# Turning four token groups between the first maxima of a fused attention and expert block

## The chip, the cores and the metric

The kernel runs on one NeuronCore of a Trainium2 chip. The engines meant below are TensorE (PE, the matrix engine, with its weight loads PEld), VectorE (DVE), ScalarE (ACT), GpSimd (POOL) and SyncE (SP), which only issues transfers. The metric is the device time of one execution in microseconds (us). The time before is 1413.76 us, the median of three runs (1411.64 to 1413.96).

## The reference

All arrays are float32. The input is 4 sequences of 1024 tokens with 256 channels, so 4096 tokens.

```python
xn = layernorm(x)                         # no weights, eps 1e-5
qkv = xn @ W_qkv + b_qkv                  # 16 heads of 16
q, k = rope(q), rope(k)
attn = softmax(q @ k.T / 4) @ v
y_att = attn @ W_out + b_out
scores = sigmoid(xn @ w_gate.T)           # 16 experts in 4 groups
# the best 2 groups by the sum of their two best scores, in them the best 4 experts,
# weights = their scores divided by their sum
routed = sum over chosen e of weight_e * (silu(xn @ w1_e.T) * (xn @ w3_e.T)) @ w2_e.T
shared = (silu(xn @ w1_s.T) * (xn @ w3_s.T)) @ w2_s.T
out = x + y_att + routed + shared
```

## The kernel before

**Tiles and groups.** The 4096 tokens are 32 tiles of 128 tokens, and four tiles make a group q of 512 tokens; there are eight groups, q = 0 to 7, two for each sequence b. Three things are done to a group in class `Norm`. `scale(q)` (L452) normalises it in place on ScalarE, in four instructions of 128x256. `turn(q, pair)` (L467) transposes two of its tiles on TensorE, four transposes of 128x128 into one PSUM bank, and ScalarE copies that bank to the transposed activations (L489). `store(q)` (L463) writes the normalised group to DRAM. Transposed groups of sequences 2 and 3 (q = 4 to 7) have only a temporary place, in buffers with the tags `oc` and `acc`, one buffer each, shared by even and odd groups, and go to DRAM from there (L542). `gate(qs)` (L494) computes the router's logits for up to four transposed groups, and `logits_of` (L513) turns them back.

**Start.** Groups 0 and 1 are normalised by VectorE and turned first; the loop at L148 then projects sequence 0 tile by tile, rotates q and k, and turns them. In the same loop ScalarE takes the sums and sums of squares of later groups (`stats_later`, L377), and GpSimd computes their scale and offset after it (`power`, L408), in the order of q.

**First maxima.** The softmax subtracts a maximum for each query that is found beforehand: `max_one` (L1237) is a product of 32 rows into a PSUM bank and a VectorE maximum over it (L1255). Four of these, one for each head of a group of heads, make a `max_round`. For the first four heads the even rounds run inside the loop and the odd rounds at L172 to L173. `max_off` (L1262) joins the halves, transposes the maxima on TensorE (tile `pmt`) and subtracts them from the queries on VectorE. Only then can the first exponentials start.

**Steps.** The rest is a run of 256 steps (L267). A step has four products `ps` with their exponentials on ScalarE (`exp_one`, L1282) and four products `pm` with their maxima for the next four heads (`max_one`). They come in two halves. Between the halves stand the step's units (`between`, L1470), which `pieces` (L544) lists: in steps 0 to 6 a further `max_round` (two in step 6), in steps 0 to 5 the two turns of group q = step + 2, the gates in steps 3 and 5, and the turning back of their logits in steps 4 and 6. After the second half come the products `av` of the step before, whole or in halves, which the flag `more` of `step` (L1446, set at L290 from `norm.gates`) decides. `moves` (L531) is called ahead of each step: it emits `scale(step + 3)`, the store of group step + 2 and, for turned groups from 4 on, the transfer of the transposed group to DRAM.

**What sets the order.** `k.pe` and `k.sp` keep the instructions of TensorE and of SP's queue in the order in which the program is written. On the other engines an instruction is ordered among others only where `keep_in_program_order` is called: on ScalarE that is so for the sums, the copies of q and k of sequence 0, the scalings of groups 2 and 3, and some later instructions. All PSUM tiles come from one pool of eight banks (L83), so a product waits until an engine has read the bank that it takes over. Routing on VectorE and GpSimd starts at step 9 with a sigmoid over the logits (L608); the zero fills of the dispatch buffer start there too.

Of the kernel before, what the change touches and what calls it, by code (L numbers as in the profile page):

```python
# [20 lines left out]
NT = B * TT  # L21
# [7 lines left out]
HALF = 512  # L29
QT = 4  # L30
# [22 lines left out]
def kernel(  # L53
# [23 lines left out]
    nc = tc.nc  # L77
# [6 lines left out]
    k = Kit(tc, banks)  # L84
# [38 lines left out]
    norm = Norm(k, att, ff, keep, logits, power)  # L123
# [44 lines left out]
    with tc.issue_after(k.rotary):  # L168
        for power_of in powers:
            power_of()  # L170
    norm.scale(2)
    for qt in range(4):  # L172
        att.max_round(0, 0, 2 * qt + 1)  # L173
    att.max_off(0, 0, 0)

    def weights():
        nc.scalar.dma_start(out=k.w1s_sb, in_=w1s.rearrange("(c p) f -> p c f", p=P))
        nc.scalar.dma_start(out=k.w3s_sb, in_=w3s.rearrange("(c p) f -> p c f", p=P))
        nc.scalar.dma_start(out=k.w2s_sb, in_=w2s.rearrange("(c p) h -> p c h", p=P))
        k.sp(wout_sb, w_out.rearrange("(c p) f -> p c f", p=P))  # L180
# [83 lines left out]

    ex = ExitStack()
    now = pieces(0)
    for step in range(STEPS):  # L267
        beside.tick()
        norm.moves(step)
        if step in k.at_step:  # L270
            with tc.issue_after(k.last_exp):
                k.at_step[step]()

        bits = []
        if routing is not None and step >= ROUTE_FROM:
            bits += [advance] * (1 if step >= PUT_FROM else 2 if k.ranking else 3)
        if step >= PUT_FROM and beside.put_next < n_put:
            assert k.slots_known
            bits[:0] = [beside.put] * 2
        if step > done.get("tiles", STEPS):  # L280
            if beside.got == 0:
                ex.close()
                beside.rows = att.rows = ctx.enter_context(
                    tc.tile_pool(name="gp", bufs=4, side="right")
                )
            for _ in range(2 if step < STEPS - 2 * TT else 1):
                bits += [beside.get, beside.add]
        then = pieces(step + 1) if step + 1 < STEPS else []

        att.step(now, bool(then) and (step + 1 > 6 or step + 1 in norm.gates), bits)  # L290
        now = then
# [4 lines left out]
class Kit:  # L296


    def __init__(self, tc, banks):
        self.tc, self.nc, self.banks = tc, tc.nc, banks  # L300
        self.last_sp = self.last_exp = None
        self.ranking = self.slots_known = False
        self.summed = self.shared_rows = 0
# [26 lines left out]
class Norm:  # L330
# [3 lines left out]
    def __init__(self, k, att, ff, keep, logits, power):  # L334
        self.k, self.nc, self.att, self.ff = k, k.nc, att, ff
        self.logits, self.power = logits, power
        self.gates = {3: (2, 3, 4, 5), 5: (6, 7)}
        self.less = keep.tile([P, NT], F32, name="less")
        self.sq = keep.tile([P, NT], F32, name="sq")
        self.x4, self.xnT, self.part, self.lg = {}, {}, {}, {}  # L340
        self.mv, self.rstd, self.off, self.scaled = {}, {}, {}, None
# [28 lines left out]
    def power_of(self, q):  # L370
        nc, ff, mv = self.nc, self.ff, self.mv[q]
        rstd = self.rstd[q] = ff.tile([P, QT], F32, name=f"rstd_{q}", tag="rstd", bufs=8)
        keep = self.k.tc.keep_in_program_order
        keep(nc.gpsimd.tensor_scalar_add(mv[:, :, 1], mv[:, :, 1], 1e-5))
        keep(nc.gpsimd.tensor_tensor(rstd, mv[:, :, 1], self.power, ALU.pow))
# [76 lines left out]
    def scale(self, q):  # L452
        nc = self.nc
        for i in range(QT):
            x = self.x4[q][:, i, :]
            scale = nc.scalar.activation(
                x, x, AF.Identity,
                bias=self.off[q][:, i : i + 1], scale=self.rstd[q][:, i : i + 1],
            )
            if q < 4:  # L460
                self.k.tc.keep_in_program_order(scale)

    def store(self, q):  # L463
# [3 lines left out]
    def turn(self, q, pair):  # L467

        nc, k = self.nc, self.k
        b, hf = divmod(q, 2)  # L470
        if hf == 0 and pair == 0 and b < 2:
            self.xnT[b] = k.xnTp.tile([P, NC_, T], F32, name=f"xnT_{b}", tag="xnT")
        if pair == 0:
            if b < 2:
                self.part[q] = self.xnT[b][:, :, hf * HALF : (hf + 1) * HALF]
            else:

                self.part[q] = self.att.one.tile(
                    [P, NC_, HALF], F32, name=f"xnTq_{q}", tag=("oc", "acc")[hf]
                )  # L480
        pt = k.bank([P, NC_, 2, P], f"pt_{q}_{pair}")
        for i in range(2):
            for c in range(NC_):
                k.pe(
                    nc.tensor.transpose(  # L485
                        pt[:, c, i, :], self.x4[q][:, 2 * pair + i, c * P : (c + 1) * P], k.ident
                    )
                )
        nc.scalar.copy(  # L489
            self.part[q][:, :, pair * 2 * P : (pair + 1) * 2 * P],  # L490
            pt.rearrange("p c i n -> p c (i n)"),
        )

    def gate(self, qs):  # L494


        nc, k = self.nc, self.k
        ps = k.bank([P, HALF], f"pg_{qs[0]}")
        for c in range(NC_):
            for j in range(4):  # L500
                k.pe(
                    nc.tensor.matmul(
                        ps[32 * j : 32 * j + 32, :],
                        lhsT=self.wg2[:, c, :],
                        rhs=self.part[qs[j % len(qs)]][:, c, :],
                        start=(c == 0), stop=(c == NC_ - 1),
                    )
                )
        lg = self.ff.tile([P, R, C], F32, name=f"lg_{qs[0]}", tag="y", bufs=3)
        self.lg[qs] = lg.rearrange("p r c -> p (r c)")  # L510
        nc.scalar.copy(self.lg[qs], ps)
# [19 lines left out]
    def moves(self, step):  # L531

        k = self.k
        q = step + 3
        if q < NT // QT:
            with k.tc.issue_after(k.last_exp or k.pace):
                self.scale(q)
        if step + 2 < NT // QT:
            self.store(step + 2)
        if 4 <= step + 1 < NT // QT:  # L540
            b, hf = divmod(step + 1, 2)
            k.sp(k.xnTd[b][:, :, hf * HALF : (hf + 1) * HALF], self.part[step + 1])  # L542

    def pieces(self, step, own):  # L544
        out = []
        if step + 2 < NT // QT:
            out += [lambda: self.turn(step + 2, 0), lambda: self.turn(step + 2, 1)]
        if own:
            out.append(own.pop(0))
        if step in self.gates:  # L550
            out.append(lambda: self.gate(self.gates[step]))
        if step - 1 in self.gates:
            out.append(lambda: self.logits_of(self.gates[step - 1]))
        return out + own
# [239 lines left out]
class Beside:  # L794
# [167 lines left out]
    def expert_units(self, ex):  # L962
# [50 lines left out]
        def pair_of(i):  # L1013
            def run():
                if i == 0:
                    for n in range(FFN_AHEAD - 1):
                        load(n)
                    turn(0)
                if i:
                    outer(i - 1)  # L1020
                if i + FFN_AHEAD - 1 < PAIRS:
                    load(i + FFN_AHEAD - 1)
                if i + 1 < PAIRS:
                    turn(i + 1)
                gus[i] = self.hidden(xTs[i], gate_and_up(i), f"r{i}")
            return run
# [543 lines left out]
```

## Time and profile before

| What | us |
|---|---|
| median of three runs | 1413.76 |
| the profiled execution, its own time | 1414.77 |
| its span, first to last instruction | 1413.1 |
| TensorE busy | 1389.0 (98%) |
| VectorE busy | 931.0 (66%) |
| ScalarE busy | 783.6 (55%) |
| GpSimd busy | 424.7 (30%) |
| mean granted TensorE clock | 0.991 |

The change lies in the first 112 us of the span. A profile row of a group gives the line, the engine, the operation and the tiles, then busy time and mean duration. A row of the windows gives, for a stretch of the span, the time for which each engine was busy and the number of its instructions, then the granted TensorE clock (1.00 is full speed), the mean busy share of the transfer engines, and GB/s. A row of the chain of waits gives start, duration and the engine and line on the path that ended last. Products are pipelined and their ends are modelled, so a busy TensorE can still be short of work; the number of its instructions in a window says more.

### The profile page before, as it was taken

How to read it: one execution, taken by the hardware profiler on the slowest of the kernel's cores; microseconds unless marked ns; L12 is line 12 of the kernel's file. 1: busy time of each engine (PE TensorE's matmuls, PEld its weight loads, DVE VectorE, ACT ScalarE, POOL GpSimd, SP SyncE). 2: the span in 40 equal slices, each digit the busy share in tenths (PEclk: the TensorE clock that was granted, in tenths of full speed). 3: DMA queues.
4: the chain of work that ended last, by engine and by line, in shares of the span. 5: the costliest groups of instructions: out<-in, count | busy, mean ns of one | idle time of the engine just before them, and what ended most of it. 6: DMA issues, size and time to landing. Idle time of an engine off the chain costs nothing.

```text
span 1413.1 us, 25832 instructions
## 1 busy us (share of the span) xinstructions
PE 1389.0 (98%) x9446; PEld 653.6 (46%) x9446; DVE 931.0 (66%) x1734; ACT 783.6 (55%) x1586; POOL 424.7 (30%) x498
## 2 busy tenths in 40 slices
PE   7899999999999999999999999999999999999998
PEld 4443333343343335566566665665664333333333
DVE  6778758778777765444555555555447988998941
ACT  4564445565555555555555555555555555555575
POOL 5401603764444454220000000002225444444400
PEclk9899999999999999999999999999999999999999
DMA  5143743413332333547666666665432434433310
GB/s 187 45 150 134 283 165 104 142 68 105 120 120 104 99 135 95 172 153 230 210 203 201 202 202 213 197 200 174 150 120 75 125 107 128 127 108 105 109 38 31
DMA packets 136670, 199.10 MB, mean 141 GB/s; under 512 B 13920, under 2 KB 99040, under 8 KB 136288
## 3 DMA queue, kind: packets, MB, share of 16 engines
q1 hardware_dynamic: 103088, 137.78, 30.7%
q0 software_dynamic: 12288, 33.57, 7.7%
q10 hardware_dynamic: 21168, 26.10, 5.3%
q8 instruction: 75, 1.23, 0.4%
q14 instruction: 51, 0.42, 0.1%
HBM read 124.01 MB, written 79.69 MB: 144 GB/s over the span
## 4 chain that ended last, share of the span: by engine, by line
PE 97%; DVE 1%; DMA 1%; ACT 1%; issue 0%; POOL 0%; ACTq 0%; POOLq 0%; DVEq 0%
PE ps L1289 20%; PE pm L1247 20%; PE av L1314 18%; PE ph_r L827 9%; PE exy L994 5%; PE ph_s L859 5%; PE pqk L1161 4%; PE py L1383 2%; PE pso L899 2%; PE pv L1161 2%; PE ext L985 2%; PE ptr L1228 2%; PE pmt L1270 1%; PE po L1338 1%; DVE mx L1255 1%; PE pt L485 1%
## 5 line engine op out<-in xcount | busy, mean ns | idle before, releaser
L1298 ACT ACTIVATE es<-ps 128x512 f32<-128x512 f32 x1024 | 554.9, 596 | 460.3 <-PE ps L1289 238.4
L1255 DVE TENSOR_REDUCE mx<-pm 128x1 f32<-128x512 f32 x1024 | 661.3, 685 | 193.9 <-PE pm L1247 139.0
L1247 PE MATMUL pm<-kT,qT 32*128 32x512 f32 x1792 | 513.1, 646 | 1.4 <-ACT kT L1233 1.4
L1289 PE MATMUL ps<-q,kT 32*128 32x512 f32 x1792 | 509.3, 643 | 3.1 <-DVE mx L1255 2.2
L1314 PE MATMUL av<-es,vv 128*32 128x512 f32 (+1 forms) x2144 | 277.3, 588 | 0.0
L1289 PEld LDWEIGHTS ps<-q,kT 32*128 32x128 f32 x1792 | 142.5, 184 | 192.5 <-ACT es L1298 135.0
L1247 PEld LDWEIGHTS pm<-kT,qT 32*128 32x128 f32 x1792 | 147.5, 185 | 67.6 <-DVE mx L1255 30.0
L835 DVE SCALAR_TENSOR_TENSOR th_r<-th_r,ph_r 128x256 f32<-128x256 f32 x72 | 30.3, 421 | 199.6 <-ACT th_r L834 199.6
L950 POOL DMA_INDIRECT xs<-rows,slot_i x128 | 124.0, 969 | 114.7 <-DVE mx L1255 101.5
L1042 POOL DMA_INDIRECT yg<-ys,slot_i x128 | 121.5, 949 | 121.8 <-DVE mx L1255 115.8
L1192 POOL TENSOR_TENSOR rot<-qk,sin_sb 128x256 f32<-128x256 f32 x56 | 39.5, 728 | 348.4 <-DVE qk L1149 348.2
L827 PE MATMUL ph_r<-xT,w 128*128 128x128 f32 x1152 | 140.5, 275 | 0.5 <-ACT xT L988 0.5
L1314 PEld LDWEIGHTS av<-es,vv 128*32 128x32 f32 x2144 | 43.1, 108 | 199.9 <-issue 178.1
L827 PEld LDWEIGHTS ph_r<-xT,w 128*128 128x128 f32 x1152 | 134.4, 192 | 0.8 <-ACT xT L988 0.7
L994 PE MATMUL exy<-w,gu_r 128*128 128x256 f32 x288 | 76.6, 388 | 0.0
L834 ACT ACTIVATE th_r<-ph_r 128x256 f32<-128x256 f32 x72 | 27.7, 384 | 82.6 <-PE ph_r L827 82.6
L1289 PE MATMUL ps<-q,qkT 32*128 32x512 f32 x256 | 72.7, 640 | 0.0
L1247 PE MATMUL pm<-qkT,qkT 32*128 32x512 f32 x256 | 72.6, 640 | 0.0
L994 PEld LDWEIGHTS exy<-w,gu_r 128*128 128x128 f32 x288 | 50.6, 190 | 28.9 <-issue 21.7
L1059 DVE SCALAR_TENSOR_TENSOR sum<-yg,wk,sum 128x256 f32<-128x256 f32 x128 | 63.6, 496 | 0.4 <-DMA yg<-ys,slot_i 0.4
L1000 ACT ACTIVATE y<-exy 128x512 f32<-128x512 f32 x72 | 43.2, 600 | 35.0 <-PE exy L994 29.9
L875 POOL TENSOR_TENSOR xb<-xb,bo_sb 128x512 f32<-128x512 f32 x16 | 20.9, 1308 | 90.4 <-DMA xb<-in_x_dram 76.4
(178 smaller groups left out, 1210.3 us busy)
## 6 DMA issues: line engine op xcount, KB each, us to landing
w<-we SPq DMA_DIRECT2D x144, 384.0 KB, 3.8
xs<-zero ACTq DMA_DIRECT2D x8, 2304.0 KB, 7.9
xg<-xs SPq DMA_DIRECT2D x72, 256.0 KB, 4.8
ys<-y SPq DMA_DIRECT2D x72, 256.0 KB, 4.7
acc<-acc SPq DMA_DIRECT2D x14, 512.0 KB, 5.2
xb<-in_x_dram SPq DMA_DIRECT2D x16, 256.0 KB, 4.2
acc<-xb SPq DMA_DIRECT2D x16, 256.0 KB, 3.2
we<-in_w_dram ACTq DMA_DIRECT2D x4, 1024.0 KB, 7.3
```

Of the source, the lines that this page charges most:

```text
L827: nc.tensor.matmul(ph[:, n, at], lhsT=w[n][:, c, :], rhs=xT[:, c, at], start=(c == 0), stop=(c == NC_ - 1),)
L859: nc.tensor.matmul(ph, lhsT=w[:, i, c * P : (c + 1) * P], rhs=self.xnT[b][:, i, at : at + SL], start=(i == 0), stop=(i == NC_ - 1),)
L950: put = nc.gpsimd.indirect_dma_start(out=k.xs, out_offset=bass.IndirectOffsetOnAxis(ap=k.slot_i[:, t, kk : kk + 1], axis=0), in_=self.rows ...
L994: nc.tensor.matmul(py[:, r, :], lhsT=gus[i][:, r * P : (r + 1) * P], rhs=got[i][1][:, r, 2 * NC_ * F :], start=True, stop=True,)
L1042: get = nc.gpsimd.indirect_dma_start(out=self.yg[:, kk, :], out_offset=None, in_=k.ys, in_offset=bass.IndirectOffsetOnAxis(ap=k.slot_i[:, ...
L1059: nc.vector.scalar_tensor_tensor(sm[:, 0, :], yg[:, kk, :], k.wk[:, t, kk : kk + 1], sm[:, 0, :], ALU.mult, ALU.add)
L1161: nc.tensor.matmul(ps, lhsT=self.xnT[b][:, c, t * P : (t + 1) * P], rhs=self.wqkv_sb[:, c, at : at + w], start=(c == 0), stop=(c == NC_ - 1),)
L1247: nc.tensor.matmul(ps, lhsT=self.qT[b, g // 2][rows, g % 2, qt * P : (qt + 1) * P], rhs=self.kT[b, g // 2][rows, g % 2, hf * HALF : (hf + ...
L1255: k.pace = nc.vector.tensor_reduce(out=self.mx_of[b, g, qt // 4][hf][:, qt % 4, j, :], in_=ps, axis=AX.X, op=ALU.max,).ins
L1289: nc.tensor.matmul(ps, lhsT=self.kT[b, g // 2][rows, g % 2, kc * P : (kc + 1) * P], rhs=self.q2[b, g, qh][rows, :], start=True, stop=True,)
L1298: k.last_exp = nc.scalar.activation(e, ps, AF.Exp, scale=DH**-0.5).ins
L1314: nc.tensor.matmul(av[32 * j : 32 * j + 32, cols], lhsT=self.vv[b][:, kc, h * VS : h * VS + 32], rhs=es[j][:, cols], start=(kc == 0), stop ...
```

## The change

Groups 2 to 5 are turned between the odd maximum rounds, ahead of the first step, and no longer in steps 0 to 3. For that their scalings come there too. Groups 6 and 7, formerly turned in steps 4 and 5, are turned in steps 2 and 3, and are scaled from steps 0 and 1. The gate over groups 2 to 5 moves from step 3 to step 1 and that over 6 and 7 from step 5 to step 4; turning back the logits follows one step later each. The scalings of groups up to 5 and the copies of the turns of groups 2 to 5 are kept in written order on ScalarE. `moves` keeps its stores of groups in the same steps; the transfers of transposed groups 4 and 5 are emitted in steps 0 and 1, those of 6 and 7 in steps 3 and 4.

```diff
     norm.scale(2)
+    norm.scale(3)
+
     for qt in range(4):
         att.max_round(0, 0, 2 * qt + 1)
+        if qt == 1:
+            norm.turn(2, 0)
+            norm.scale(4)
+        if qt == 2:
+            norm.turn(2, 1)
+    for q in (3, 4):
+        for pair in range(2):
+            norm.turn(q, pair)
+    norm.scale(5)
     att.max_off(0, 0, 0)
+    for pair in range(2):
+        norm.turn(5, pair)
...
-        self.gates = {3: (2, 3, 4, 5), 5: (6, 7)}
+
+        self.turns, self.gates = {2: 6, 3: 7}, {1: (2, 3, 4, 5), 4: (6, 7)}
...
-            if q < 4:
+            if q < 6:
                 self.k.tc.keep_in_program_order(scale)
...
-        nc.scalar.copy(
+        copy = nc.scalar.copy(
             self.part[q][:, :, pair * 2 * P : (pair + 1) * 2 * P],
             pt.rearrange("p c i n -> p c (i n)"),
         )
+        if 2 <= q < 6:
+            k.tc.keep_in_program_order(copy)
...
-        q = step + 3
+        q = step + 6
         if q < NT // QT:
             with k.tc.issue_after(k.last_exp or k.pace):
                 self.scale(q)
         if step + 2 < NT // QT:
             self.store(step + 2)
-        if 4 <= step + 1 < NT // QT:
-            b, hf = divmod(step + 1, 2)
-            k.sp(k.xnTd[b][:, :, hf * HALF : (hf + 1) * HALF], self.part[step + 1])
+        q = step + 4 if step < 2 else self.turns.get(step - 1)
+        if q:
+            b, hf = divmod(q, 2)
+            k.sp(k.xnTd[b][:, :, hf * HALF : (hf + 1) * HALF], self.part[q])
...
-        if step + 2 < NT // QT:
-            out += [lambda: self.turn(step + 2, 0), lambda: self.turn(step + 2, 1)]
+        if step in self.turns:
+            out += [lambda i=i: self.turn(self.turns[step], i) for i in range(2)]
```

## The prediction

> **What bounds the kernel now.** I read the page's rows by slices first (a dip in TensorE's clock in slices 2 and 4), then the chain of waits from 46 us on, then the windows, and last the timelines of the engines up to 112 us. Rows of the chain, with start and duration:
>
> ```profile
> 49.20 9.65 DVE mx L1255 x16
> ...
> 59.12 1.13 PE pmt L1270 x4
> ...
> 60.34 0.70 DVE q L1275
> ...
> 61.08 1.22 PE ps L1289
> ...
> 63.17 1.90 PE pt L485 x8
> 65.07 2.63 PE pm L1247 x9
> ```
>
> To be seen: before the first step VectorE's sixteen odd maxima (0.604 us each) set the end for 9.65 us, and TensorE waits. From 61.08 on TensorE is the path, and the turns are pieces of it: 1.90 us in step 0, then 1.02 to 1.03 in each of steps 1 to 5 (rows at 70.77, 77.15, 83.52, 90.72 and 98.43). The change moves turns from the second stretch into the first. The windows show a second loss. I cut them at 3.41 us because the six jumps of the clock up to 180 us (53.65, 67.3, 128.8, 135.6, 176.6, 180.0) lie whole multiples of that apart.
>
> ```profile
> 46.82:50.24 3.42, 2.22 (x17) 1.01 (x18) 2.26 (x5) 3.42 (x11) 3.09 (x14) 1.00 0.00 0
> 50.24:53.65 3.41, 3.41 (x13) 1.60 (x12) 3.41 (x7) 1.94 (x4) 3.19 (x22) 1.00 0.61 207
> 53.65:57.06 3.41, 2.53 (x5) 0.72 (x4) 3.41 (x7) 0.00 (x0) 3.00 (x8) 0.51 0.62 183
> 57.06:60.48 3.42, 1.12 (x4) 0.72 (x4) 2.11 (x5) 0.00 (x0) 0.67 (x2) 0.50 0.00 0
> 60.48:63.89 3.41, 2.81 (x12) 1.30 (x13) 1.21 (x3) 0.70 (x2) 0.00 (x0) 0.50 0.00 0
> 63.89:67.30 3.41, 3.41 (x18) 2.00 (x20) 0.82 (x3) 1.54 (x3) 0.00 (x0) 0.50 0.00 0
> 67.30:70.72 3.42, 3.42 (x17) 1.20 (x9) 3.42 (x7) 2.51 (x6) 0.00 (x0) 0.99 0.29 79
> ```
>
> The first pair behind the stretch's length is TensorE, busy time and instructions; the first number after the last bracket is the granted clock. With 13 starved matmuls in a window the clock falls to half; it stays there for four windows, which hold the pmt transposes and nearly all of step 0.
>
> **Part 1, the entry.** TensorE's added work is the turns of groups 2 to 5: 32 transposes, eight in 1.02 us, 4.1 us. All but those of group 5 are hidden under the 9.65 us of maxima. Do they starve VectorE through the eight banks? The product of maximum 14 would take over the bank of turn (2,0). ScalarE copies that bank behind eight scalings of 0.515 us (timeline: eight in 4.12 us from 48.06), so it is free at 52.8. I put the product at 54.0, and its maximum is due at 57.7: no stall. If a copy were 4 us later there would be one.
>
> ScalarE now has a chain of its own: 16 scalings (8.2 us) and eight copies (0.54 to 0.59 us, 4.5 us), from 48.06 to 60.8 if nothing gaps. Placed link by link: the copies of groups 3 and 4 end about 58.2 (their turns get banks as maxima 9 to 11 end, 55.2 to 56.4), and group 5's scaling runs to 60.3. TensorE in its fixed order does pmt at 59.12, 0.6 us at full clock, then turn (5,0), waits until 60.3, does turn (5,1) and is free at 60.85. So the wait on ScalarE takes the place of the half-speed pmt (1.13 us) and the subtraction behind it (0.70): first ps at 60.9 against 61.08. Queued behind that wait are all of step 0's products, hence the exponentials and VectorE.
>
> The unknown here is where ScalarE's scaling of group 6 lands: it is not kept in order and step 0's pace is a VectorE instruction. Behind the first exponentials it costs nothing; ahead of group 5's it costs four scalings, 2.06 us (a turn can't be late by more). Its nearest row is group 3's scaling, emitted in the same way in step 0 before, but kept in order, and that ran far ahead. I take 0 and keep 2.06 for the range. Its offset is no limit: GpSimd has it at 56.2, group 4's at 52.6, and 4 is scaled at 52.8.
>
> **Part 2, step 0.** Before, the first maximum started at 63.23, 2.15 us after the first product, and the tenth ended at 71.99, with VectorE idle for 2.59 us in between. At full clock the same product-to-maximum delay was 1.20 us (75.69 to 76.89). Afterwards: 60.9 + 1.20 = 62.1, then ten maxima back to back (1.29 + 4.88 us by VectorE's rows) end at 68.25. TensorE's products for them come to about 4.6 us, so VectorE paces. Gain **3.7 us**. Of this the turn's 1.90 us is one part and the clock the rest; neither adds in full, because VectorE is next.
>
> **Part 3, steps 1 to 6.** Five turns were left there, two remain: 3 x 1.02 = **3.1 us** off TensorE's path. Gates (1.85 us each) and logits (0.59 us each) are moved only; they count the same before and after. Can VectorE follow? Between 72 and 111 us its waits on TensorE are 5.7 + 3.5 = 9.2 us, so a saving of 3.1 has room. If steps without any extra unit are held up by VectorE (eight maxima, 4.9 us) a third of it is lost, 1 us; if the better spread of gates helps, 0.5 more comes.
>
> **Part 4, what costs nothing, and its cover.** On SP's queue the transfer of transposed group 4 now waits for a copy at 58.2, and group 3's store, group 5's transfer, w_out and group 4's store queue behind it. Such a transfer lands in 3.0 to 3.9 us; w_out is first read at 120.77, and the temporary buffer of group 4, needed again by group 6 in step 2, is read out by about 62 and by the gate in step 1. Without that cover turn 6 would wait. The stores of x that free these buffers first were issued at 14.4 and 15.9. Logits done a step sooner bring nothing: the first reader is the sigmoid at 122.76. From step 7 on instructions, their order and the zero fills are placed by step number, so the rest moves as a block; the path there is TensorE nearly everywhere.
>
> **Sum.** 3.7 + 3.1 = 6.8 us off the profiled execution's own 1414.77, i.e. 1407.97. That execution was 1.0 above the median 1413.76, so the forecast for a median is 1413.76 - 6.8 = **1407.0**.
>
> **A rule against the change.** Part of the gain needs the clock to stay up while TensorE transposes. First the row: the window 63.89:67.30 restored the clock at its end, though turns fill it until 65.07, that is 35% of it. The window before it, idle until 61.08 (17%), did not, nor did 128.74:132.16, which had no full-array transposes and was filled from 129.5 on (78%). So 65% of other work restored what 78% could not: transposes must count. The Trainium skill, "TensorE: Matmul & The Clock Gate", Part 4: PE-mode transpose, says the opposite: full clock does not engage for transposes, which do not count as busy in the same way. By the rule the clock falls at about 53.65 as before, the turns take 8 us in the entry, first ps comes near 62.3, step 0 runs at half speed as before, and only its turn and the three later ones are won: 1.90 + 3.1 - 1.2 = 3.8 us, 1410.0. By the row 1407.0. I go with the row, since the filled windows 50.24 and 53.65 would get eight and sixteen transposes more; 57.06:60.48 with some eight or twelve in all stays doubtful, and a fall there would cost at most 1.7 us.
>
> **Rivals.**
>
> (B) *Smaller gain, 1410.0.* The clock falls before step 0 after all, by the rule above, or group 6's scaling comes first (6.8 - 2.1 = 4.7, so 1409.1). For it: the skill, and the unordered scaling. Against it: the windows.
>
> (C) *Slower, 1417.2.* Clock falls in steps 0 to 6. There TensorE, once ahead of VectorE, waits for banks: twelve products, 24 matmuls, in 4.9 us make about 16.7 a window. At 17 the clock stayed, at 13 it fell; the skill's page, "A second HAM failure mode: psum-queue depth-cycling", describes such oscillation. A fall lasts two windows (128.8 to 135.6) and costs half of 6.8 us, 3.4. Two falls give back the gain; from three it is slower: -6.8 + 3 x 3.4 = +3.4. Against it: gates, turns and av fill TensorE in steps 1 to 6, and in the window 104.85:108.26, paced by VectorE with 20 matmuls, the clock stayed.
>
> (D) *No change, 1413.8.* The gain is lost at a fixed transfer further on: the chain has 6.92 us from 164.83 for loading xb. If the load ended at a set time, all 6.8 us would go there. Against it: the load is issued by its step, as are the fills beside it.
>
> (E) *The turns are not out of the path*, because they starve the maxima: 4.1 us back into the entry, 1411.1. Against it: the bank count of part 1.
>
> **How the numbers follow.** Forecast 0.60, B 0.16, E 0.03, D 0.09, C 0.12. A measurement of this kernel can tell about 0.2%, 2.8 us, from no change: faster means below 1410.9, slower above 1416.6. Faster: the forecast and most of B, 0.74. Same: D, E and the rest of B, 0.14. Slower: C, 0.12. The range: the forecast's own bounds are 6.8 + 0.5, and 6.8 - 2.1 - 1.0; the clock's falls at 128.8 and 176.6 cost 3.4 and 1.7 us and may not recur, since the shift puts other work into those windows. So down to 1403.5. Up I go to 1412.0, which takes in B and E and leaves out C and D.
>
> **What would show it.** Right: maxima L1255 still unbroken for 9.65 us from about 49.2; turns L485 of groups 2 to 4 inside it; clock 1.00 from 50 to 68; first ps at 60.5 to 61.5; VectorE unbroken for its first ten maxima of the steps; step 7 about 6.8 us sooner, and the same lead at the end. Wrong: gaps in the maxima (E), half clock between 53 and 68 (B) or again up to 110 (C), first ps after 62.5 (group 6 first), a lead that vanishes between 120 and 180 (D).

## The result: slower, with the profile after

The changed kernel takes 1419.45 us (median of five runs, 1417.33 to 1422.17) against 1411.78 for the kernel before (now five runs, 1411.53 to 1413.96). The ratio is 1.0046 (1.0032 to 1.0061). The forecast was 1407.0 with a range of 1403.5 to 1412.0; the kernel got slower, not faster. Ratios are given with their 95% intervals and can differ in the last digits from the quotient of the two medians. The profiled execution took 1417.33 us; its span is 1415.6.

The place to look is the same stretch as before. First the chain of waits of the changed kernel up to the first products of the odd rounds (start, duration, engine, line):

```profile
51.36 0.97 POOL rstd L389
...
53.95 0.97 POOL rstd L433
...
55.55 1.02 POOL rstd L433
...
56.64 0.21 POOL off L435
...
56.87 1.09 ACT x L470 x2
57.96 0.52 ACT qT L1250 x2
58.49 0.55 ACT kT L1250 x2
...
60.02 0.97 ACT x L470 x2
...
61.85 3.80 PE pm L1264 x16
```

Before, this stretch of the path belonged to VectorE's maxima. Now GpSimd is on it, which the forecast had set aside ("Its offset is no limit"): it computes the scale and offset of one group after another (L389, L433, L435), and as soon as the offset of group 6 is there, ScalarE scales `x`, that is group 6, and only then copies q and k. ScalarE's timeline (start, duration, then idle time before the row and what ended it) says why:

```profile
45.24 0.51 ACT L413 ACTIVATE other<-x,less 128x256 f32<-128x256 f32 x1
45.64 0.20 ACT L413 ACTIVATION_READ_ACCUMULATOR other<-x,less 128x1 f32 x1
56.87 1.09 ACT L470 ACTIVATE x<-x,off,rstd 128x256 f32<-128x256 f32 x2 [11.03 <-POOL off L435]
57.87 0.62 ACT L1250 COPY qT<-ptr 128x256 f32<-128x256 f32 x2
58.38 0.65 ACT L1250 COPY kT<-ptr 128x256 f32<-128x256 f32 x2
...
61.93 4.07 ACT L470 ACTIVATE qkT<-qkT,off,rstd 128x256 f32<-128x256 f32 x8
```

In the kernel before, nothing stood between the squares and those copies, and the scalings of groups 2 and 3 followed them:

```profile
47.54 0.71 ACT L1233 COPY kT<-ptr 128x256 f32<-128x256 f32 x2
48.06 4.12 ACT L456 ACTIVATE qkT<-qkT,off,rstd 128x256 f32<-128x256 f32 x8
```

In the changed kernel one half of group 6's scaling stands ahead of the copies of q and k of each of the last two tiles of sequence 0. ScalarE does nothing for 11.03 us, although the transposes that those copies read were done by 47.4. The list of waits shows what hung on it (waiting engine and line, engine waited for, total, times, longest):

```profile
DVE mx L1272 <- PE pm L1264: 15.2, 1, 15.2
PEld pm L1264 <- ACT kT L1250: 14.7, 1, 14.7
PE pm L1264 <- ACT kT L1250: 14.4, 1, 14.4
ACT x L470 <- POOL off L435: 11.0, 1, 11.0
```

TensorE can't start the odd rounds without k, and VectorE can't take maxima. The sixteen maxima themselves are as unbroken as before, only later, and so is the start of the steps (VectorE's timeline):

```profile
63.96 9.66 DVE L1272 TENSOR_REDUCE mx<-pm 128x1 f32<-128x512 f32 x16 [15.16 <-PE pm L1264]
...
74.66 0.69 DVE L1292 TENSOR_TENSOR q<-qT,pmt 128x512 f32<-128x512 f32 x1 [0.82 <-PE pmt L1287]
76.86 8.46 DVE L1272 TENSOR_REDUCE mx<-pm 128x1 f32<-128x512 f32 x14 [1.51 <-PE pm L1264]
```

The odd maxima start at 63.96 and not at 49.18. After that what the forecast spoke of is there: fourteen maxima without a gap, where the kernel before had gaps of 2.59 and 0.90 us:

```profile
67.11 4.88 DVE L1255 TENSOR_REDUCE mx<-pm 128x1 f32<-128x512 f32 x8 [2.59 <-PE pm L1247]
72.89 3.68 DVE L1255 TENSOR_REDUCE mx<-pm 128x1 f32<-128x512 f32 x6 [0.90 <-PE pm L1247]
```

The subtraction of the maxima from the queries (L1292 here, L1275 before) comes 32 times in the run and serves as a time mark for comparing executions. The table has its start in each profiled execution, as a distance from the kernel before; the experiments are described below.

| subtraction | before, us | changed | keep6 | late67 | early6 | power6 | dummy | dummy2 |
|---|---|---|---|---|---|---|---|---|
| first (entry) | 60.34 | +14.32 | +0.09 | -0.59 | +13.91 | +6.44 | -0.04 | -0.07 |
| second (step 7) | 114.31 | +7.20 | -7.02 | -7.70 | +13.37 | -0.68 | -1.23 | -2.86 |
| fourth | 168.01 | +4.96 | -9.28 | -8.35 | +14.69 | -0.25 | -0.89 | -5.12 |
| fifth | 211.98 | +2.48 | -11.72 | -7.65 | +16.28 | -1.06 | -1.73 | -6.00 |
| last | 1365.78 | +2.54 | -11.69 | -7.83 | +16.10 | +1.61 | -1.51 | -3.04 |

Read down the column of the changed kernel: 14.32 lost at the entry, 7.12 won back in steps 0 to 7, 4.72 more won between 128 and 212 us. The last part I don't count to the change: in the profiled execution before, the clock fell twice there (128.8 and 176.6), in the changed one it did not fall again between 66 us and the end, and such falls differ from one execution to the next. The runs below fit that: keep6, whose clock did not fall there either, wins 4.70 us in that stretch, and late67, with three windows of 3.41 us at half clock there like the kernel before, wins none. The medians differ by 7.7 us, near the 7.2 of the second row.

### The profile page after: what moved, and what is told of

Its sections match the earlier page's. It is cut to its first block, busy times and chain, and to the rows that moved or that the text cites. A ratio compares the mean times of both kernels' runs of the same rounds, so it can differ in the third digit from the quotient of the medians.

```text
span 1415.6 us, 25845 instructions
## 1 busy us (share of the span) xinstructions
PE 1381.8 (98%) x9454; PEld 651.5 (46%) x9454; DVE 929.3 (66%) x1734; ACT 784.5 (55%) x1586; POOL 425.1 (30%) x498
## 3 DMA queue, kind: packets, MB, share of 16 engines
q8 instruction: 75, 1.23, 0.4%
## 4 chain that ended last, share of the span: by engine, by line
PE 96%; POOL 1%; DVE 1%; ACT 1%; issue 0%; DMA 0%; ACTq 0%; POOLq 0%; DVEq 0%
PE ps L1306 20%; PE pm L1264 20%; PE av L1331 18%; PE ph_r L844 9%; PE exy L1011 5%; PE ph_s L876 5%; PE pqk L1178 4%; PE py L1400 2%; PE pso L916 2%; PE ext L1002 2%; PE pv L1178 2%; PE ptr L1245 2%; PE po L1355 1%; PE pmt L1287 1%; PE pf L1388 1%; PE pt L499 1%
## 5 line engine op out<-in xcount | busy, mean ns | idle before, releaser
L1264 PE MATMUL pm<-kT,qT 32*128 32x512 f32 x1792 | 506.9, 643 | 14.4 <-ACT kT L1250 14.4
```

What stands on the lines that cost most here:

```text
L1264: nc.tensor.matmul(ps, lhsT=self.qT[b, g // 2][rows, g % 2, qt * P : (qt + 1) * P], rhs=self.kT[b, g // 2][rows, g % 2, hf * HALF : (hf + ...
```

## Experiments

**Keep group 6 in order (keep6).** One character of the changed kernel:

```diff
-            if q < 6:
+            if q < 7:
                 self.k.tc.keep_in_program_order(scale)
```

> The changed kernel, with group 6's scaling kept in written order on ScalarE as well, behind the copies of group 5's turn. Theory Q (a queue on ScalarE: unordered, this scaling stands ahead of the last copies of q and k and waits there for GpSimd's offset): the wait of 11.0 us is gone, the odd maxima start near 49 instead of 63.96, the lead won in steps 0 to 6 (7.1 us) stays, so 1411.8 - 7 = about 1405 (1401 to 1408). Theory T (the loss comes from the moved turns and copies themselves): the odd maxima still start late or have gaps, and the time stays at 1415 or more. Theory K (the clock): it falls in steps 0 to 6, and the time is 1410 to 1417.

Measured: 1404.89 us, ratio to the kernel before 0.9952 (0.9939 to 0.9966). In ScalarE's timeline the copies of q and k follow the squares at once, and group 6's scaling comes behind the copies of group 5's turn:

```profile
47.58 0.67 ACT L1250 COPY qT<-ptr 128x256 f32<-128x256 f32 x2
48.09 0.70 ACT L1250 COPY kT<-ptr 128x256 f32<-128x256 f32 x2
48.62 4.14 ACT L470 ACTIVATE qkT<-qkT,off,rstd 128x256 f32<-128x256 f32 x8
...
60.90 1.23 ACT L503 COPY xnTq<-pt 128x512 f32<-128x512 f32 x2
62.02 2.07 ACT L470 ACTIVATE x<-x,off,rstd 128x256 f32<-128x256 f32 x4
64.00 1.06 ACT L1315 ACTIVATE es<-ps 128x512 f32<-128x512 f32 x2
```

Its odd maxima start at 49.74. So theory Q held in time and in place; T and K did not.

**Scale groups 6 and 7 a step later (late67).**

```diff
-        q = step + 6
-        if q < NT // QT:
+        q = step + 5
+        if 6 <= q < NT // QT:
             with k.tc.issue_after(k.last_exp or k.pace):
```

> The changed kernel, with the scalings of groups 6 and 7 emitted one step later (steps 1 and 2), where a ScalarE exponential to place them behind exists. Theory Q: about 1404.5 (1401 to 1408), as in the run that keeps group 6 in order or up to 1.5 us below it, since 2.06 us of scaling no longer stand before the first exponentials. Theory T: 1415 or more. If the order of group 6 is what counts, both ways of mending it give the same time within 1.5 us.

Measured: 1405.72 us, ratio 0.9944 (0.993 to 0.9957). Two different mends of the order give the same time within the runs' spread (late67 moves group 7's scaling by a step too). Here the first exponentials start at 61.91, ahead of group 6's scaling, and in keep6 at 64.00, behind it, yet from the first to the second subtraction both win 7.1 us: with VectorE as the pace, 2.07 us of scaling before the first exponentials cost nothing. VectorE's timeline of late67:

```profile
49.05 9.66 DVE L1272 TENSOR_REDUCE mx<-pm 128x1 f32<-128x512 f32 x16 [1.15 <-PE pm L1264]
58.74 0.19 DVE L1283 TENSOR_TENSOR mx<-mx,mx 128x16 f32<-128x16 f32 x1
59.75 0.69 DVE L1292 TENSOR_TENSOR q<-qT,pmt 128x512 f32<-128x512 f32 x1 [0.82 <-PE pmt L1287]
61.95 8.46 DVE L1272 TENSOR_REDUCE mx<-pm 128x1 f32<-128x512 f32 x14 [1.52 <-PE pm L1264]
```

**The early scaling alone (early6).** The kernel before, with nothing moved but this:

```diff
         q = step + 3
-        if q < NT // QT:
+        for q in {0: (3, 6), 3: ()}.get(step, (q,) if q < NT // QT else ()):
             with k.tc.issue_after(k.last_exp or k.pace):
                 self.scale(q)
```

> The kernel before, with one thing of the change alone: group 6's scaling is emitted in step 0 instead of step 3, unordered. No turn, gate or copy is moved. Theory Q: ScalarE waits about 11 us for GpSimd ahead of the last copies of q and k, the odd maxima start 14 us later (near 63.5), and the whole is slower by 10 to 15 us: 1422 to 1427. Theory T: nothing happens, 1412.

Measured: 1429.77 us, ratio 1.0118 (1.0103 to 1.0134). A row each of ScalarE's and of VectorE's timeline:

```profile
56.01 1.09 ACT L456 ACTIVATE x<-x,off,rstd 128x256 f32<-128x256 f32 x2 [11.02 <-POOL off L421]
```

```profile
63.10 9.66 DVE L1255 TENSOR_REDUCE mx<-pm 128x1 f32<-128x512 f32 x16 [15.19 <-PE pm L1247]
```

The same wait to 0.01 us, and the same late entry, without a turn, a gate or a copy moved. The total is some 3 us above the range expected. That part does not come from the entry: the delay is 13.91 us at the first subtraction and 13.37 at the second, and grows to 16.28 by the fifth. In that last stretch this execution had four windows of 3.41 us at half clock (141.83 to 148.66 and 189.62 to 196.44), the kernel before three; half a window, some 1.7 us, is explained by that, the rest stays open.

**An earlier offset (power6).** The changed kernel with ScalarE's order as it was, and GpSimd taking group 6 first:

```diff
-        for q in range(2, last):
+        for q in (6, *range(2, 6), 7):
             powers.append(lambda q=q: power(q))
```

> The changed kernel, with GpSimd computing group 6's scale and offset ahead of those of groups 2 to 5 (its constants then come before all of them in its queue). ScalarE's order is the changed kernel's, with group 6's scaling ahead of the last copies of q and k. Theory Q: what costs the time is how late the offset is. GpSimd is free of the rotation at about 45.9, its constants take some 4 us and the offset 1.4, so the wait on ScalarE ends near 51.5 and not at 56.8; the odd maxima start at 57 to 60, between 49 and 64, and the time is about 5 us below the changed kernel: 1412 to 1416. A rival, that the place of the scaling alone costs what was lost, whatever it waits for, keeps 63.9 and 1419.

Measured: ratio 0.998 (0.9973 to 0.9988), 1416.36 us; it ran on another chip, on which the kernel before took 1419.79, so only the ratio compares. A row of ScalarE's timeline:

```profile
49.00 1.09 ACT L470 ACTIVATE x<-x,off,rstd 128x256 f32<-128x256 f32 x2 [4.17 <-POOL off L435]
```

The odd maxima start at 56.09. The direction is as theory Q has it, the size was missed: the rotation ended at 44.8 and not at 45.9, GpSimd's constants took 2.6 us and not 4, the wait ended at 49.0 and not at 51.5, and the gain over the changed kernel (1.0046 to 0.998, some 9 us) is larger than the 5 expected. At the first subtraction 6.9 us less of wait made 7.9 us less of delay. So the larger part of what the place in the queue costs is the wait, and that is set by when the operand comes.

**Does the clock count transposes? (dummy, dummy2)** The kernel before with spare transposes behind each odd round; nobody reads them.

```diff
         att.max_round(0, 0, 2 * qt + 1)
+        spare = k.bank([P, NC_, 4, P // 2], f"spare_{qt}").rearrange("p c i n -> p (c i n)")
+        for i in range(8):          # dummy2: 8 if qt < 3 else 22
+            k.pe(nc.tensor.transpose(
+                spare[:, i % 4 * P : (i % 4 + 1) * P],
+                norm.x4[1][:, i % 4, : P], k.ident,
+            ))
     att.max_off(0, 0, 0)
```

> The kernel before, with eight spare transposes of 128x128 behind each of the four odd maximum rounds, 4.1 us of TensorE work whose results nobody reads. If transposes keep the clock up (the reading of the row): granted clock 1.00 from 50 to 68 us, step 0 at full speed, the first maxima of step 1 some 3 us sooner, 1408 to 1410. If they do not count (the skill's rule): the clock falls near 53.7 as before and returns near 67, 1412 to 1415.

> The kernel before with the spare transposes, 22 instead of eight behind the last of the odd rounds, so that TensorE is at work until the maxima are transposed. In the run with eight the clock held from 50 us and fell at 61.6 for one window, after some 2.3 us of idling. If filled windows are what holds it, it now stays at 1.00 up to 68, step 0 keeps its turn (1.0 us at full clock) and runs at full speed: the subtraction for the second half of the first heads (at 114.31 before) is 2.3 to 3 us sooner, which is the clock's share of the gain; the time is 1409 to 1411. If transposes hold the clock only in part, it falls again at about 61.

Measured: dummy 1411.51 us, ratio 0.998 (0.9966 to 0.9994); dummy2 ratio 0.9959 (0.9939 to 0.998), 1412.99 us on the second chip. Windows of dummy, columns as in the prediction:

```profile
51.40:54.80 3.40, 3.40 (x28) 2.11 (x24) 3.40 (x7) 1.22 (x3) 3.18 (x19) 1.00 0.83 276
54.80:58.20 3.40, 2.48 (x17) 1.45 (x16) 3.40 (x7) 0.00 (x0) 2.91 (x7) 1.00 0.40 115
58.20:61.60 3.40, 1.22 (x12) 0.73 (x12) 1.93 (x4) 0.00 (x0) 0.05 (x1) 1.00 0.00 0
61.60:65.00 3.40, 3.40 (x20) 2.09 (x16) 1.29 (x2) 2.26 (x4) 0.00 (x0) 0.54 0.00 0
```

and of dummy2:

```profile
58.20:61.60 3.40, 1.82 (x18) 1.06 (x16) 1.90 (x4) 0.00 (x0) 0.05 (x1) 1.00 0.00 0
61.60:65.00 3.40, 3.40 (x32) 1.98 (x24) 2.02 (x4) 2.05 (x4) 0.00 (x0) 1.00 0.00 0
```

In dummy the clock holds past 53.65, where it fell before, and falls for one window at 61.86, behind the window 58.20:61.60 with its 12 instructions; in dummy2, which has 18 there, it does not fall. So transposes do keep the clock up, which the rule denied. VectorE shows it too: it waits 0.82 us for the transposes of the maxima in both, against 1.28 before. Dummy2 brought what the row let expect. Dummy fell short: the one window at half clock took in the first turn of step 0, so it won 1.2 us by the second subtraction where 3 were expected. Dummy2 won 2.9. That is what the clock is worth in steps 0 to 6, measured with no turn moved. Dummy2's ratio is better than that; it had no fall near 128 either.

## Why the prediction was wrong, step by step

**The step that failed** is the unknown of part 1: "where ScalarE's scaling of group 6 lands". The prediction took 0, "and keep 2.06 for the range", with "a turn can't be late by more" and "its offset is no limit: GpSimd has it at 56.2". It cost 14.3 us at the entry. Early6 shows that this one edit makes that delay by itself, and keep6 and late67 that undoing it alone takes the delay away.

Two errors lie in that passage. The bound from above was the work of the four scalings, but an instruction ahead of others in ScalarE's queue costs its wait too, here 11.03 us. And the offset at 56.2 was held against the place where the prediction wanted the scaling, near 60, not against the earliest place where it could stand, which is behind group 6's own squares at about 45. From there to 56.2 is 11 us. The parts of the delay, against late67: 11.0 of wait, 2.0 of scaling ahead of the copies, 0.9 by which the squares ended later in this execution (45.84 against 44.96), and about 0.95 because the clock had fallen in the gap (from the first product to the first maximum 2.11 us, against 1.16). Together 14.9, and the odd maxima start 14.9 later. The row that spoke of it was cited and set aside: group 3's scaling before, emitted in step 0 as well, ran at 50.1, while the instruction it was to be issued behind ran at 58.2. So that hint (`issue_after` in `moves`) placed nothing on ScalarE when it named an instruction of VectorE; in step 0 there is no exponential yet. In late67, where it names an exponential, the scaling came behind the first exponentials, at 64.95. No run changed the hint alone.

The Trainium skill, "TensorE: Matmul & The Clock Gate", in the notes on queue depths under Part 1, says that ScalarE and VectorE are strict FIFO. The trace agrees: ScalarE sat idle from 45.84 to 56.87 with the inputs of its next copies ready by 47.4.

**The entry otherwise** was right: maxima unbroken for 9.66 us, turns between them, first product at 60.75 in late67, forecast 60.9. **Part 2** was right: ten maxima in a row from 61.95, which ends the tenth 4.0 us sooner than before; forecast 3.7. **Part 3** came out near: late67 leads by 7.70 us at the second subtraction, so 3.7 us fall to the rest of the steps, forecast 3.1; no run shows how much of it the three turns are. **Part 4**: no wait on SP's transfers or on the temporary buffers shows in the changed kernel between 62 and 125 us.

**Rule or row**: the row was right, by dummy and dummy2. The prediction's working of it (65% against 78%) did not yet prove it: in late67 the window 121.37:124.78 brought the clock back with 17 instructions and no full-array transpose. The window that the prediction called doubtful was the one that failed in dummy, with 12 instructions; with the moved turns it held 16 in keep6 (58.53:61.95) and 19 in late67 (56.52:59.93), and the clock stayed.

**The rivals**: B's clock part and E did not happen (in late67 and keep6 the granted clock is 1.00 from 50 to 68 us, and the maxima have no gap). C, the only slower one, named the wrong mechanism: from 68 to 120 us the clock was 1.00 in the changed kernel, keep6 and late67 alike. D did not happen: the lead of keep6 and late67 lasts to the end. What happened was a form of B's second half, group 6's unordered scaling coming first; the prediction had it as a sign of being wrong, priced at 2.1 us where it cost 14.3.

Keep6 and late67 beat both kernels. Of the 7 to 8 us that late67 leads by, some 2.9 are the clock's, if what dummy2 won with the turns in place can be carried over; the rest is left for the turns and for the smoother steps, which was not taken apart further.

## What to carry to other kernels

When an instruction is emitted earlier and nothing holds its place in its engine's queue, find the earliest place at which it may land and bound its cost by the time from there until its last operand arrives, plus its own work; work alone bounds nothing. Ask also who stands behind it: here two copies that fed TensorE. An ordering hint that names another engine's instruction may place nothing, as here, so keep such instructions in order expressly, or emit them where an instruction of their own engine exists to follow.

## What the runs showed of the hardware

Full-array transposes between sparse products were enough to hold TensorE's clock: with eight of them behind each odd round it stayed at 1.00 until 61.86 us, where it had fallen at 53.65 without them. It is decided in windows of about 3.4 us: up to 230 us, every stretch at half clock in these traces lasts a multiple of 3.41 us (13.65, 6.83 and 3.41 us in the kernel before). In the entry, windows with at most 13 instructions of TensorE let it fall and windows with 16 or more did not. But the number of instructions is not the rule. Two windows with the same busy time, the first from power6 and the second from dummy, went the other way: the clock stayed behind the first, with 11, and fell behind the second, with 17.

```profile
152.23:155.65 3.42, 2.83 (x11) 0.92 (x9) 3.42 (x7) 1.20 (x3) 2.77 (x4) 1.00 1.04 377
150.61:154.02 3.41, 2.83 (x17) 0.90 (x16) 3.41 (x7) 1.02 (x3) 2.48 (x3) 1.00 1.04 379
```

What decides, and why the clock falls near 128 and 176 us in some executions and not in others, was not settled. The executions of late67 lay between 1403.27 and 1406.96 us, with a mean granted clock from 0.999 to 0.996 in the same order, so much of this kernel's spread goes with the clock. And two chips differed by 0.5% for the kernel before (1413.26 and 1419.79 us).
